# Which slot of a recurrent step takes filler work: a one-core scheduler change in a four-layer residual block

## The chip, the cores and the metric

The kernel runs on one core of one Trainium2 chip. Its time is the device time of one execution in microseconds, and the figure for a kernel is the median over several executions. The profile is one further execution, recorded by the hardware profiler.

## The reference

The input x has shape (8, 512, 256): 8 sequences of 512 time steps with 256 features, and there is one condition vector of 256 features per sequence. Four layers follow each other, each added to its input:

```
x = x + L0(x, cond)   # 8 routed experts (top 2 by a sigmoid router), one shared expert
x = x + L1(x, cond)   # Haar wavelet down and up, gated: reduces to a scale per sequence and feature
x = x + L2(x, cond)   # x@base_down + low rank of rank 8, gelu, base_up + low rank
x = x + L3(x, cond)   # a GRU over time:
   Z = sigmoid(xz + H@Whz.T + bhz);  R = sigmoid(xr + H@Whr.T + bhr)
   H_tilda = tanh(xh + (R*H)@Whh.T + bhh)
   H = Z*H + (1-Z)*H_tilda;          Y = H@Whq.T + bhq
```

All is float32. Layers 0 to 2 work on each time step alone; L3 is 512 steps that each need the step before.

## The kernel before

The 512 time steps are cut into 16 windows of 32 steps (256 columns: 8 sequences by 32 steps). For each window the lower layers (0 to 2) are a list of small jobs, made by `window_jobs` (routing by `route`): a PE job, here called a unit, is four matmuls that fill the four 32-column groups of the array, nearly always with 256 columns. ACT, DVE and POOL jobs stand between the units. Layer 3 then runs over chunks of 16 steps.

The order of all engines is fixed while the program is written (`tc.manual_schedule()`). The loop over steps emits the recurrent chain of each step, and at fixed places it calls `jobs.fill(engine, now, most)`, which takes up to `most` jobs that are ready by the planner's own clock (`STEP` = 2.43 us for a step, a time for each job in `TAKES`, a margin of 0.2 us). The program's order is then final: an engine that meets a job whose input is late stands still, with all that is queued behind it.

One step emits on PE, in this order:

1. eight matmuls into `grh` from the state `s_h` (reset gate, called R below) and eight into `gz` from `s_h` (update gate),
2. the first slot: units of `jobs.fill("PE", now + 0.5, ...)`, and in every second step four matmuls of the input projection of a later step (`wx` into `grh`, called P below),
3. eight matmuls into `grh` from `s_rh` (the candidate, called H below),
4. the second slot: in the other steps four projection matmuls into `gz`, called `Zx` below, and then units of `jobs.fill("PE", now + 1.44, ...)`.

Between them ACT makes `r`, `z` and `c`, and DVE transposes them, makes `s_rh` and, with two scans at line 1372, the new state `s_h`. After the scans DVE takes one or two jobs of the lower layers, and POOL one. ACT takes one after `z` and one after `c`. The next step's R waits for the scans. So the time from one pair of scans to the next is the length of a step.

The function `behind(s)` says whether more units are left than a straight line over the steps allows. Before the change the first slot takes a unit if `behind(s)`, the second takes two in every second step if `behind(s)`, and one otherwise. Output products of the GRU (`hist` times `Whq`, lines 453 and 1178, made by `output_jobs`) of chunks 0 to 11 are urgent jobs; those of the last four chunks (`HELD` = 12) lie in the queue `jobs.last`, which `fill` opens when no other PE job is left.

The activations `sig` of the lower layers lie in one ring of three buffers, `r_sig`, and a ring is given out in the order of asking. PSUM banks are rings too: `hp` has two, `low`, `acc` and `misc` one each. An `hp` unit that starts a bank therefore waits for the readers of the bank's former content.

Of the kernel before, what the change touches and what calls it, by code (L numbers as in the profile page):

```python
# [16 lines left out]
P = 128  # L17
B, T, C = 8, 512, 256
KC = C // P
# [7 lines left out]
NT = B * WS  # L27
# [109 lines left out]
class Jobs:  # L137


    def __init__(self):  # L140
        self.queues = {e: [] for e in TAKES}
        self.urgent = {e: [] for e in TAKES}
        self.last = {e: [] for e in TAKES}
        self.small = {e: [] for e in TAKES}
        self.clock = {e: 0.0 for e in TAKES}
        self.now = 0.0

    def add(self, eng, fn, deps=(), lazies=(), takes=None, queue=None, lag=0.0):
        job = Job(eng, fn, list(deps), list(lazies), takes, lag)
# [7 lines left out]
    def fill(self, eng, now, most, ahead=40, then=None, of=None):  # L157

        n = 0
        while n < most:  # L160
            last = [] if self.left("PE") else self.last[eng]
            for q in of or (self.urgent[eng], self.queues[eng], last):
                job = next((j for j in q[:ahead] if j.ready(now)), None)
                if job is not None:
                    break
            else:
                return n
            q.remove(job)
            made = job.emit(now)
            if then is not None:  # L170
                then(made)
            now += job.takes
            n += 1
        return n
# [25 lines left out]
def cond_resid_kernel(  # L200
# [29 lines left out]
    nc = tc.nc  # L230
# [31 lines left out]
    def ring(name, shape, bufs, space=None):  # L262
        return Ring(pool_of("r_" + name, bufs, space), name, shape, bufs)
# [4 lines left out]
    r_acc = ring("acc", pair, 1, PSUM)  # L268
    r_m = ring("misc", pair, 1, PSUM)
    r_sig = ring("sig", [P, NT], 3)  # L270
    r_lin = ring("lin", [P, NT], 2)
    r_g = ring("g", [P, NT], 6)
    r_gl = ring("gl", [P, NT], 3)
# [36 lines left out]
    jobs = Jobs()  # L310
# [31 lines left out]
    xw, xg, got_x = [], [], []  # L342
# [122 lines left out]
    def window_jobs(w, routed, xt, via_pool=False):  # L465
# [74 lines left out]
        for m in range(HC):  # L540
            h, sig, lin, g = bank(), Lazy(r_sig), Lazy(r_lin), Lazy(r_g)
# [28 lines left out]
        for e2 in range(0, E, 2):  # L570
            h = bank()
            for n in range(2):
                e = e2 + n
                j = hidden(h, n, lambda k, e=e: rw1_sb[:, k, e, :], got_rw1)
# [109 lines left out]
        ends = adapted(mid_ps, 0, x2, A_DOWN, done, True)  # L684
        mids = []
        for m in range(KC):
            sig = Lazy(r_sig)

            a = add(
                "ACT",  # L690
                lambda m=m, sig=sig: nc.scalar.activation(
                    sig.get(), mid_ps.get()[:, m], AF.Erf, scale=0.5 * RSQRT2
                ),
                [ends[m]],
                [mid_ps, sig],
            )
            mids.append(
                add(
                    "DVE",
                    lambda m=m, sig=sig: stt(  # L700
                        mid.get()[:, m], sig.get(), 1.0, mid_ps.get()[:, m], ALU.add, ALU.mult
                    ),
                    [a],
                    [mid_ps, sig, mid],
                )
            )
# [25 lines left out]
    def pe(fn, deps, lazies=(), takes=0.3):  # L732
        return jobs.add("PE", fn, deps, lazies, takes)
# [7 lines left out]
    def flat(z):  # L741
        t = z.get()
        return t if len(t.shape) == 2 else t.rearrange("p a b -> p (a b)")
# [45 lines left out]
    def route(ws, tiles, psum, via_pool, behind=()):  # L789

        first, n, J = ws[0], len(ws), B
        assert n == NQ and WS == 32
        takes = 0.18 + J * E / 1000.0
        logits = Lazy(psum)

        def products():
            for k in range(KC):
                for i, w in enumerate(ws):
                    nc.tensor.matmul(
                        flat(logits)[ts(i, 32), :NT],  # L800
                        rout_sq[:, k],
                        xw[w][:, k],
                        start=(k == 0),
                        stop=False,
                        skip_group_check=True,
                    )

        d = pe(
            products, [*(got_x[w] for w in ws), got_rout_sq, *behind], [logits], 0.45
        )  # L810

        def rt(name, last=E):
            return tiles.tile([P, J, last], F32, name=f"{name}_{first}")

        def bc(t):
            return t.broadcast_to([P, J, E])


        logit, s, sel, rank = rt("logit"), rt("s"), rt("sel"), rt("rank")
        turned = tiles.tile([P, B, 32], F32, name=f"turned_{first}")  # L820
        rb3 = rbias.rearrange("p (o e) -> p o e", o=1)
        pr3 = prio.rearrange("p (o e) -> p o e", o=1)

        def turn(dst, src):
            nc.vector.transpose(dst, src.rearrange("p (b q) -> p b q", q=32))

        d = dve(lambda: turn(turned, flat(logits)[:, :NT]), [d], [logits], 0.45)
        d = dve(lambda: tt(logit, turned[:, :, :E], tbias, ALU.add), [d, got_tbias], (), takes)
        d = act(lambda: nc.scalar.activation(s, logit, AF.Sigmoid), [d])

        def then(fn):
            nonlocal d
            queue = jobs.queues if via_pool else jobs.small
            d = jobs.add("DVE", fn, [d, got_rbias], (), takes, queue)

        then(lambda: tt(sel, s, bc(rb3), ALU.add))
        hot = []
        for i in range(2):
            top, best, one = rt(f"top{i}", 1), rt(f"best{i}", 1), rt(f"one{i}")
            then(lambda top=top: nc.vector.tensor_reduce(top, sel, AX.X, ALU.max))  # L840
            then(lambda top=top: tt(rank, sel, bc(top), ALU.is_equal))
            then(lambda: tt(rank, rank, bc(pr3), ALU.mult))
            then(lambda best=best: nc.vector.tensor_reduce(best, rank, AX.X, ALU.max))
            then(lambda one=one, best=best: tt(one, rank, bc(best), ALU.is_equal))
            hot.append(one)
            if i == 0:
                then(lambda one=one: stt(sel, one, -3.0e38, sel, ALU.mult, ALU.add))
        both = hot[0]
        den, some, rden = rt("den", 1), rt("some", 1), rt("rden", 1)
        then(lambda: tt(both, hot[0], hot[1], ALU.add))  # L850
        then(lambda: tt(s, s, both, ALU.mult))
        then(lambda: nc.vector.tensor_reduce(den, s, AX.X, ALU.add))
        then(lambda: nc.vector.tensor_scalar(some, den, EPS_GATE, None, ALU.is_gt))
        then(lambda: nc.vector.tensor_scalar(den, den, EPS_GATE, None, ALU.add))
        then(lambda: nc.vector.reciprocal(rden, den))

        then(lambda: stt(rden, rden, 0.5, some, ALU.mult, ALU.mult))
        then(lambda: nc.vector.tensor_scalar(some, some, -0.25, 0.25, ALU.mult, ALU.add))
        then(lambda: tt(s, s, bc(rden), ALU.mult))
        then(lambda: tt(both, both, bc(some), ALU.mult))  # L860
        square = squares[first // EARLY % 2]
        then(lambda: tt(square[:, :, :E], s, both, ALU.add))
        cT = tiles.tile([P, NT], F32, name=f"cT_{first}")
        d = dve(
            lambda: turn(
                cT.rearrange("p (b q) -> p b q", q=32), square.rearrange("p b q -> p (b q)")
            ),
            [d],
            (),
            0.45,  # L870
        )
        made = []
        for i in range(n):
            eng = "SP" if not via_pool else "ACT" if i else "POOL"

            def put(i=i, eng=eng):
                {"SP": nc.sync, "ACT": nc.scalar, "POOL": nc.gpsimd}[eng].dma_start(
                    out=comb_d[ws[i]], in_=cT[32 * i : 32 * i + E]
                )

            made.append(jobs.add(eng, put, [d], (), 0.9 if eng == "POOL" else 0.5, lag=LAG))
        return made
# [203 lines left out]
    with (  # L1086
# [158 lines left out]
        def behind(s, by=0):  # L1245
            return (
                any(j.done is None for j in ends[1])
                or jobs.left("PE") > all_left * (LAST - s) / (LAST + LEAD) + by
            )

        def late(s):

            return not jobs.left("PE")

        copying = None
        z_bias = None
        biased = []
# [6 lines left out]
        for c in range(NTC):  # L1264
            hist = hists[c]
            gates = upcoming
            for t in range(TC):
# [72 lines left out]
                if 2 * GS <= ahead < T:  # L1340
# [4 lines left out]
                    part = parts.pop(0)  # L1345
                    if ahead % WS == WS - 1:
                        projected[ahead // WS].done = now + 1.0
                jobs.fill("PE", now + 0.5, 1 if behind(s) or late(s) else 0)
                if part is not None and ahead % 2 == 0:
                    part()  # L1350
                    part = None
# [5 lines left out]
                cand, act_c = gate(rh[:, n, 1], AF.Tanh, "c", KC)  # L1357
                if part is not None:
                    part()
                two = behind(s, 8) or ahead % 2 == 0 and behind(s)  # L1360
                jobs.fill("PE", now + 1.44, 2 if two else 1)
                if bias_parts and t >= 7:
                    biased.append(bias_parts.pop(0)())
                    if not bias_parts:
# [100 lines left out]
```

## Time and profile before

| what | value |
|---|---|
| median of three runs | 1330.2 us (1329.89, 1330.2, 1331.93) |
| the profiled execution's own time | 1334.46 us |
| its span, first to last instruction | 1332.2 us |
| mean granted TensorE clock | 0.984 |
| PE busy | 1183.3 us (89%) |
| DVE busy | 914.9 us (69%) |
| ACT busy | 507.3 us (38%) |
| POOL busy | 149.3 us (11%) |
| first and last scan start (DVE, line 1372) | 71.1 us and 1326.5 us |

The profiled execution is 4.3 us above the median of the runs, so its parts cannot be taken for those of a typical run without a thought. Busy shares say little here: PE is busy nine tenths of the time, but much of that is filler that lies in gaps of the recurrent chain. What counts is how long a step takes, and which steps take longer than the others.

### The profile page before, as it was taken

How to read it: one execution, taken by the hardware profiler on the slowest of the kernel's cores; microseconds unless marked ns; L12 is line 12 of the kernel's file. 1: busy time of each engine (PE TensorE's matmuls, PEld its weight loads, DVE VectorE, ACT ScalarE, POOL GpSimd, SP SyncE). 2: the span in 40 equal slices, each digit the busy share in tenths (PEclk: the TensorE clock that was granted, in tenths of full speed). 3: DMA queues.
4: the chain of work that ended last, by engine and by line, in shares of the span. 5: the costliest groups of instructions: out<-in, count | busy, mean ns of one | idle time of the engine just before them, and what ended most of it. 6: DMA issues, size and time to landing. Idle time of an engine off the chain costs nothing.

```text
span 1332.2 us, 88576 instructions
## 1 busy us (share of the span) xinstructions
PE 1183.3 (89%) x39016; PEld 704.9 (53%) x39016; DVE 914.9 (69%) x6255; ACT 507.3 (38%) x3403; POOL 149.3 (11%) x228
## 2 busy tenths in 40 slices
PE   8999989999898998989898988888888888988885
PEld 4565555555555555555454554545454554555554
DVE  5267777777776767666676767667676766767665
ACT  2143433343343434334343434434343443433332
POOL 3310111101010110101011010101101010110000
PEclk8999999999999999999999999999999999989997
DMA  9910001101010000201000010100001000000111
GB/s 338 330 51 13 4 6 44 44 5 36 5 41 15 20 20 4 52 4 28 12 21 20 4 36 4 28 12 20 20 4 36 4 4 4 5 4 4 36 36 19
DMA packets 41586, 46.44 MB, mean 35 GB/s; under 512 B 27472, under 2 KB 31088, under 8 KB 40048
## 3 DMA queue, kind: packets, MB, share of 16 engines
q1 hardware_dynamic: 38304, 38.31, 9.6%
q8 instruction: 304, 4.98, 1.5%
q0 software_dynamic: 1184, 2.31, 0.6%
q14 instruction: 82, 0.67, 0.2%
q10 hardware_dynamic: 1712, 0.16, 0.1%
HBM read 36.45 MB, written 4.33 MB: 31 GB/s over the span
## 4 chain that ended last, share of the span: by engine, by line
PE 68%; DVE 17%; ACT 8%; issue 5%; DMA 1%; POOL 0%; DVEq 0%; ACTq 0%; POOLq 0%
PE grh L1115 34%; PE hp L453 13%; PE acc L453 8%; DVE rT L1295 6%; DVE d L1295 5%; PE gz L1115 5%; ACT r L1281 5%; PE low L453 4%; ACT c L1281 3%; PE misc L453 3%; DVE s_h L1372 2%; DVE s_rh L1312 2%; DMA brow<-in_bias_rows_dram 0%; DMA bc<-comb_d 0%; PE misc L1023 0%
## 5 line engine op out<-in xcount | busy, mean ns | idle before, releaser
L1281 ACT ACTIVATE r<-grh 128x32 f32<-128x32 f32 x1024 | 146.3, 195 | 439.8 <-PE grh L1115 439.8
L1295 DVE STREAM_TRANSPOSE rT<-r 128x32 f32<-128x32 f32 x1024 | 156.0, 190 | 225.6 <-ACT r L1281 221.6
L1115 PE MATMUL grh<-wh,s_h 128*32 128x64 f32 x8192 | 223.8, 226 | 75.4 <-DVE s_h L1372 74.2
L1115 PEld LDWEIGHTS grh<-wh,s_h 128*32 128x32 f32 x8192 | 145.0, 110 | 274.4 <-DVE s_h L1372 271.2
L1115 PE MATMUL grh<-wh,s_rh 128*32 128x64 f32 x8192 | 223.1, 227 | 52.0 <-DVE s_rh L1312 29.8
L1281 ACT ACTIVATE c<-grh 128x32 f32<-128x32 f32 x1024 | 146.3, 195 | 310.0 <-PE grh L1115 307.6
L1115 PEld LDWEIGHTS grh<-wh,s_rh 128*32 128x32 f32 x8192 | 141.6, 109 | 201.5 <-DVE s_rh L1312 198.9
L1295 DVE STREAM_TRANSPOSE d<-c 128x32 f32<-128x32 f32 x1024 | 156.5, 192 | 119.3 <-ACT c L1281 113.5
L1115 PE MATMUL gz<-wh,s_h 128*32 128x64 f32 x8192 | 212.1, 221 | 1.2 <-issue 1.2
L1115 PEld LDWEIGHTS gz<-wh,s_h 128*32 128x32 f32 x8192 | 155.3, 111 | 1.7 <-issue 1.6
L453 PE MATMUL hp<-x,sw_sb 128*32 128x256 f32 x2016 | 151.8, 389 | 1.7 <-ACT sig L546 1.1
L594 POOL TENSOR_TENSOR g<-gl,bc 128x256 f32<-128x256 f32 x128 | 93.6, 733 | 518.1 <-DVE s_h L1372 355.6
L453 PE MATMUL hp<-x,rw_sb 128*32 128x256 f32 x2016 | 149.6, 380 | 2.3 <-ACT sig L578 1.1
L453 PE MATMUL acc<-g,rw_sb 128*32 128x256 f32 x2048 | 150.2, 379 | 1.6 <-POOL g L594 1.1
L1372 DVE TENSOR_TENSOR_SCAN s_h<-d,d 128x16 f32<-128x16 f32 x1024 | 145.3, 183 | 0.0
L1312 DVE TENSOR_TENSOR s_rh<-rT,s_h 128x8 f32<-128x8 f32 x1024 | 133.1, 167 | 0.0
L1295 DVE STREAM_TRANSPOSE zT<-z 128x64 f32<-128x64 f32 x512 | 121.6, 238 | 1.1 <-ACT z L1281 1.1
L1281 ACT ACTIVATE z<-gz 128x64 f32<-128x64 f32 x512 | 121.0, 236 | 1.9 <-PE gz L1115 1.4
L1115 PE MATMUL grh<-wx,xt 128*32 128x128 f32 x2048 | 106.8, 276 | 3.3 <-ACT r L1281 3.3
L1386 ACT COPY hist<-s_h 128x16 f32<-128x16 f32 x512 | 105.9, 207 | 0.5 <-DVE s_h L1372 0.5
L1324 DVE TENSOR_TENSOR d<-zT,s_h 128x16 f32<-128x16 f32 x512 | 90.8, 177 | 17.6
L1325 DVE TENSOR_SCALAR d<-zT 128x16 f32<-128x16 f32 x512 | 86.8, 170 | 0.0
(151 smaller groups left out, 1193.4 us busy)
## 6 DMA issues: line engine op xcount, KB each, us to landing
bc<-comb_d SPq DMA_DIRECT2D x56, 256.0 KB, 3.2
w<-in_w_dram SPq DMA_DIRECT2D x8, 1024.0 KB, 12.6
out_dram<-x SPq DMA_DIRECT2D x14, 256.0 KB, 3.2
x<-in_xT_dram SPq DMA_DIRECT2D x2, 1536.0 KB
rw_sb<-in_rw_dram SPq DMA_DIRECT2D x2, 1024.0 KB
bc<-comb_d POOLq DMA_DIRECT2D x8, 256.0 KB, 8.4
sw_sb<-in_sw_dram SPq DMA_DIRECT2D x3, 512.0 KB, 6.3
wsq_a<-in_sq_a_dram SPq DMA_DIRECT2D x1, 1280.0 KB
```

The source lines that it names most:

```text
L453: nc.tensor.matmul(out[ts(j, 32)], lhs[:, ts(j, 32)], rhs, start=start, stop=False, skip_group_check=True,)
L594: lambda gl=gl, g=g, e=e: nc.gpsimd.tensor_tensor(g.get(), gl.get(), bcs[e // 2].get()[:, e % 2], ALU.mult),
L1115: nc.tensor.matmul(out[ts(j, 32)], lhs, rhs[:, ..., ts(j, FQ)], start=start, stop=False, skip_group_check=True,)
L1281: nc.scalar.activation(x, y, func)
L1295: ins = nc.vector.transpose(dst.rearrange("p i u b -> p i (u b)"), src.rearrange("p (i r) -> p i r", r=32),)
L1312: prod = tt(s_rh[u][:, k, u, :], rT[:, k, u, :], h[:, k], ALU.mult)
L1324: tt(d1[:, :, u, :, 1], zT[:, :, u, :], h, ALU.mult)
L1325: nc.vector.tensor_scalar(d0[:, :, :, 1], zT[:, :, u, :], -1.0, 1.0, ALU.mult, ALU.add)
L1372: new = nc.vector.tensor_tensor_scan(s_h[v][:, k, v].rearrange("p b w -> p (b w)"), d0[:, k].rearrange("p b w -> p (b w)"), d1[:, k, u].re ...
L1386: nc.scalar.copy(hist[:, :, t, :], s_h[v][:, :, v, :, 1])
```

## The change

Four things are done.

- The activations of layer 2 (the `sig` of `mid`) get a ring of their own with two buffers, `r_mid_sig`; they no longer take turns in `r_sig`.
- The router's product for four windows, one PE job of eight matmuls, becomes two jobs of four, one for each half of the features.
- The number of units of a slot depends on how many PE jobs are ready by the planner's clock. The first slot takes one if the kernel is behind and more than one is ready, else none; once all PE jobs of the lower layers are out, it takes an output unit only if more of them are left than steps. The second takes two if the kernel is behind and more than two are ready, else one. While window 1 is unfinished, and when the end has begun, the ready count isn't asked for.
- The end begins when the last product of layer 0 is out, not when no PE job is left: `fill` then opens `jobs.last`, and the held output units are spread over both slots of the remaining steps.

```diff
+        self.ending = lambda: not self.left("PE")
...
-            last = [] if self.left("PE") else self.last[eng]
+            last = self.last[eng] if self.ending() else []
...
+    r_mid_sig = ring("mid_sig", [P, NT], 2)
...
-            sig = Lazy(r_sig)
+            sig = Lazy(r_mid_sig)
...
-        def products():
-            for k in range(KC):
-                for i, w in enumerate(ws):
...
+        def products(k):
+            for i, w in enumerate(ws):
...
+        d = None
+        for k in range(KC):
+            deps = [*(got_x[w] for w in ws), got_rout_sq, *behind, d]
+            d = pe(lambda k=k: products(k), deps, [logits], 0.45)
...
+        def first_slot(s, at):
+
+            if any(j.done is None for j in ends[1]) or jobs.ending() and jobs.left("PE"):
+                return 1
+            if jobs.left("PE"):
+                return 1 if behind(s) and jobs.ready("PE", at + 1.0) > 1 else 0
+            return 1 if len(jobs.last["PE"]) > T - s else 0
+
+        def second_slot(s, at):
+
+            if not jobs.left("PE"):
+                return 1
+            two = behind(s, 8) or (s + 5) % 2 == 0 and behind(s)
+            if two and (any(j.done is None for j in ends[1]) or jobs.ending()):
+                return 2
+            return 2 if two and jobs.ready("PE", at + 1.0) > 2 else 1
+
+        jobs.ending = lambda: l0_ends[-1].done is not None
...
-                jobs.fill("PE", now + 0.5, 1 if behind(s) or late(s) else 0)
+                jobs.fill("PE", now + 0.5, first_slot(s, now + 0.5))
...
-                two = behind(s, 8) or ahead % 2 == 0 and behind(s)
-                jobs.fill("PE", now + 1.44, 2 if two else 1)
+                jobs.fill("PE", now + 1.44, second_slot(s, now + 1.44))
```

More of the change, by code (lines that the diff above doesn't have):

```diff
@@ L794, in route @@
         logits = Lazy(psum)
-        def products():
-            for k in range(KC):
-                for i, w in enumerate(ws):
[L799 to L810, printed above, removed]
+        def products(k):
+            for i, w in enumerate(ws):
+                nc.tensor.matmul(
+                    flat(logits)[ts(i, 32), :NT],
+                    rout_sq[:, k],
+                    xw[w][:, k],
+                    start=(k == 0),
+                    stop=False,
+                    skip_group_check=True,
+                )
+        d = None
+        for k in range(KC):
+            deps = [*(got_x[w] for w in ws), got_rout_sq, *behind, d]
+            d = pe(lambda k=k: products(k), deps, [logits], 0.45)
         def rt(name, last=E):
@@ L1249, in behind @@
             )
-        def late(s):
-            return not jobs.left("PE")
+        def first_slot(s, at):
[12 more added lines that the diff above has]
+        jobs.ending = lambda: l0_ends[-1].done is not None
         copying = None
```

## The prediction

> **What bounds the kernel now.** I read the cores' line first, then the page, the waits, a timeline of the scans, and tables of stretches. The page says PE 89% busy, but the waits say what the time hangs on:
>
> ```profile
> span 1332.2 us, 88576 instructions
> ACT r L1281 <- PE grh L1115: 439.8, 509, 3.3
> ACT c L1281 <- PE grh L1115: 307.6, 487, 1.5
> PEld grh L1115 <- DVE s_h L1372: 271.2, 501, 1.0
> PEld grh L1115 <- DVE s_rh L1312: 198.9, 479, 0.7
> ```
>
> PE to ACT to DVE to PE, about 500 times each: the chain of one step goes round the engines, and the filler lies in PE's gaps. So I took the length of every step, from the timeline of the line 1372 scans, end to end: 1255.3 us for 511 steps, and the commonest length is 2.417 us. A step with two lone units in its second slot and one in its first has the median 2.417, and so has a step with none. Filler is free as long as it is on time. 511 x 2.417 is 1235.1, so **20.2 us of the profiled run are excess**, and the change can win no more than that and the ends. I sorted the excess by step:
>
> - 5.4 us: steps 80-81, 142-143, 206-207 and 457-459, each just after a light stretch.
> - 5.6 us: steps 55-56, 72, 74, 97, where PE waits for "issue".
> - 1.6 us: steps 508 to 511.
> - 7.6 us: some sixty steps of 0.04 to 0.6 each, where a slot is too full or a unit late.
>
> The first group and the third have one cause. Stretches of 3.41 us, two pairs, then the two at the end:
>
> ```profile
> 421.96:425.37 3.41, 1.76 (x90) 1.17 (x81) 2.72 (x19) 1.84 (x12) 0.00 (x0) 1.00 0.03 5
> 425.37:428.79 3.42, 3.42 (x70) 2.44 (x74) 1.81 (x12) 0.74 (x6) 0.00 (x0) 0.50 0.02 5
> 578.97:582.39 3.42, 1.76 (x90) 1.17 (x81) 2.73 (x19) 1.84 (x12) 0.00 (x0) 1.00 0.02 5
> 582.39:585.80 3.41, 3.41 (x68) 2.41 (x72) 1.75 (x11) 0.64 (x5) 0.00 (x0) 0.50 0.00 0
> ...
> 968.09:971.50 3.41, 1.79 (x76) 1.24 (x76) 2.85 (x20) 1.64 (x11) 0.00 (x0) 1.00 0.02 5
> ...
> 1312.84:1316.25 3.41, 1.74 (x80) 1.26 (x80) 1.94 (x15) 1.15 (x10) 0.00 (x0) 1.00 0.04 10
> 1316.25:1319.67 3.42, 2.28 (x82) 2.01 (x85) 2.02 (x16) 1.03 (x8) 0.00 (x0) 0.50 0.00 0
> ```
>
> The columns are length, PE busy, weight loads, DVE, ACT, POOL, granted clock, DMA. A stretch with PE busy 1.74 to 1.76 of 3.41 us is followed by one at half clock; one with 1.78 or 1.79 is not. The clock's changes lie on a grid of 3.413 us. A step of the bare recurrence has 1.1 us of PE, 1.55 in a stretch: under the line. In matmul columns, counting both passes of float32, it has 3072 a step, the drops follow stretches of 5312 or less, and the lightest middle stretch without one has 5376. Two empty slots in a row, of steps 141 and 142, let the clock fall, if the grid lies badly.
>
> Two more costs, a slot too full and the instruction stream:
>
> ```profile
> 137.24 1.05 PE L799 MATMUL misc<-x,rout_sq 128*32 128x256 f32 x16
> 138.10 0.61 PE L453 MATMUL hp<-x,sw_sb 128*32 128x256 f32 x8
> 138.53 0.41 PE L1115 MATMUL grh<-wh,s_h 128*32 128x64 f32 x16
> ...
> 198.77 1.78 SPq L485 DMA_DIRECT2D bc<-comb_d  x4
> ...
> 205.64 1.07 PE L453 MATMUL low<-u,low_out 128*32 128x256 f32 x16 [2.15 <-issue]
> ```
>
> The scan before R ended at 138.24 and R began at 138.53, 0.3 late (on time it begins 0.04 before that end), behind router plus unit. In the third case four 256 KB transfers are issued together, no 16 KB packet of the instruction queue starts from 195.5 to 203.2 (3.5 to 5 us apart else), and PE runs dry.
>
> **The change part by part.** I counted slots in the two programs' orders. The matmuls are the same 19512, none is added.
>
> *Empty slots.* Before, 41 second slots hold no unit (20 of them with Zx), after 18, and most pairs of empty slots (21-22, 45-46, 51-52, 75-76, 109-111, 140-142, 172-174, 204-206, 236, 267, 300, 365, 397, 455-459) now hold a unit each. What was put there was taken from full slots. I slid the 3.413 us grid in 64 positions over each order, counted columns, and took 5340 as the line. Before: 2.1 half-clock stretches up to step 500, on average over the positions; after: 0.2 (step 469 alone). The profiled run drew five (two of them one pair), for 5.38 us: 1.1 each. So the part is 5.4 less 0.2 = **-5.2 in this execution**, and -2.1 in a typical run: three stretches fewer are also most of what sets the 1334.46 above the 1330.2.
>
> Here the Trainium skill speaks against the change. "TensorE: Matmul & The Clock Gate", section "What's actually happening", has the PE fall back after at least one idle window of about 3.4 us, and the section on oscillation asks for no PE gap above that. The longest gap in the loop is 2.15 us, and before 425.37 PE was never idle for a microsecond. By that rule empty slots cost nothing, the part is 0, and the end gains nothing. The rows show half clock at half activity, so I go with them; by the rule the sum would be 3.3 less.
>
> *End.* Steps 506-507 before hold little, and the last outputs are 32 columns wide: half clock from 1316.25. After, outputs begin at step 459 and last with a unit or two a step to 507, then 64-column units in 508-509. Sliding the grid: 3.0 half-clock stretches from step 500 before, 0.8 after. 1.56 x 0.8 / 3.0 leaves 0.4: **-1.2**. Behind the last scan the same three instructions stand on ACT, PE, DVE and the same two stores: 0, or -0.3 with the clock up. DVE's last-slice adds and SP's stores move with the outputs; SP has nothing else by then, the last inputs being in.
>
> *Full slots and late units.* By pattern, from the step lengths:
>
> - Router. Three steps of eight router matmuls plus a unit (28, 58, 88): +0.297, +0.299, +0.299. After, two of the three still have both halves in one slot, without a third unit; the third is split. A slot of two units costs 0: -0.9. A second job instead of one adds nothing on other engines.
> - Two output units with Zx before P: 29 steps of 0.047 (R at 1249.60 is such a one, 0.06 late). Nine are left: -0.94.
> - Zx, `acc`, `hp` and then a `gl` that waits for that `hp`: seven steps of 0.18 to 0.28, 1.67 together, since the next first slot's `hp` waits for `gl`, and P and H stand behind it. One is left: -1.43.
> - The same with `hp` before `acc`, six steps, 0.31; two left: -0.2. Without Zx, ten steps of 0.094; seven left: -0.28.
>
> That is -3.75. Against it stand pairs that the trace doesn't show: a slot of two with a `mid_sig` after it, `gl` behind two `hp` units, three DVE jobs in one gap (one step). Below nothing is possible only by what these replace, already counted. Upper bound: a dozen such places at 0.25, the late `gl`'s price, is 3. I take 1.2, as most of them have the distance of places that cost 0: **-2.5**. The three claims matmuls' step (4, +0.55) stays.
>
> *Prologue.* PE has two units more before step 0. One (0.43 x 2 for both halves) goes ahead of `misc<-mid`, where PE stood 0.38 waiting for `mid`: +0.4 on the way to `xt`. Behind it, a wait of 0.57 for `sig` (66.29) goes, and P, which starts at 67.61 though `xt` was there at 66.24, comes sooner. Bounds -1.0 and +0.5, **-0.3**.
>
> *Instruction stream and transfers.* SP's order: the second routing's four stores and the four `bc` loads still go together, at steps 54-55 in place of 52-54; so the 3.15 us stall and its half-clock follower (0.62) I leave in place. The other three (0.48, 0.53, 0.86) sit behind single loads in the busiest steps; which steps get them shifts. **0**; bounds -5.6 (none) and +2 (the burst lasts 6.35 us, a dry PE of 4 in place of 2.15).
>
> *Sum* against the profiled execution: 1334.46 - 5.2 - 1.2 - 2.5 - 0.3 = 1325.3. Against the median: 1330.2 - 2.1 - 1.2 - 2.5 - 0.3 = 1324.1. After the change the draw of the grid matters little, so both should name one number: **1324.5**.
>
> **The rivals.**
>
> - *First-slot units wait.* A unit in the first slot stands ahead of H, on the chain. After, 40 first-slot `hp` units need a bank whose reader is DVE's job of the gap just before, 25 one whose reader is ACT's job after `c`; before 45 and 10. At 0.25 each, all 65 would be +16, less the 1.7 already there: 1338. It beats the gain from 25 waits on, and is slower by 0.2% from 35 on. For: the seven steps named. Against: those are 7 of 45; a first DVE job ends 0.45 into the step and the slot starts at 0.5. 7%.
> - *A draw.* A typical run has few drops, the burst's stall grows by 2 and new waits reach 3: 1330.2 - 3.3 - 3.75 + 3 + 2 = 1328. 13%.
> - *The clock follows the skill's rule*, or another line: -2.8, 1327.4. 10%, half of it within 0.2%.
> - *The split router does not split*: true in two of three steps, but the gain comes from the third unit's absence. No time of its own.
>
> **How the numbers follow.** The main case has 70%. A measurement of this kernel can tell 0.2%, 2.7 us. Low end: no new waits (-1.2) and half of the stalls gone (-3): 1320. High end: new waits at 3 (+1.8), a longer burst (+2), prologue at +0.5 (+0.8): 1329. This holds the draw and the skill's rule. Faster (under 1327.5): 70% and most of the rule's tenth and a bit of the draw, 0.80; same 0.13; slower 0.07.
>
> **What would show it.** Right: granted clock near 1.00 from 75 to 1310 save after the burst; scans 2.417 apart around steps 141, 205, 457; no 0.3 at the router's steps; the output steps at 2.417. Wrong: waits of H for `gl` or `sig` in the first slot in dozens of steps; half-clock stretches in spite of filled slots; a stall at step 55 of over 4 us; a first scan later than 72.

## The result, and the profile after

The changed kernel takes 1320.17 us (median of 4 runs) against 1330.86 us for the kernel before: ratio 0.9911, interval 0.9899 to 0.9924. A second set of runs of it gave 0.9899 (0.9883 to 0.9915); all its 9 runs have a median of 1320.6 us. The forecast of 1324.5 us had the direction and most of the places right, and took the gain for half of what it is: 5.7 us below the median that it started from, against 10.7 us measured.

The two profiled executions are 1334.46 and 1319.46 us. First the span from the page after, and four rows of the waits of after (us in total, times, longest):

```profile
span 1317.7 us, 88546 instructions
```

```profile
ACT r L1298 <- PE grh L1117: 426.6, 505, 7.3
PEld grh L1117 <- DVE s_h L1388: 308.7, 511, 1.0
ACT c L1298 <- PE grh L1117: 307.8, 501, 1.0
...
PEld grh L1117 <- DVE s_rh L1329: 190.8, 480, 0.8
```

The chain still goes round PE, ACT, DVE, PE, and the common step is 2.417 us as before. But PE now waits for the new state in 511 steps and for 308.7 us, where before it waited in 501 and for 271.2: it arrives early more often, because fewer slots run over.

The stretches of 3.41 us around steps 141 and 142, and those at the end (length, PE busy, weight loads, DVE, ACT, POOL, granted clock, DMA):

```profile
412.80:416.21 3.41, 3.06 (x112) 1.81 (x108) 2.68 (x19) 1.74 (x12) 0.00 (x0) 1.00 0.02 5
416.21:419.63 3.42, 3.05 (x107) 1.59 (x102) 2.58 (x17) 1.39 (x9) 0.00 (x0) 1.00 0.02 5
...
1307.09:1310.51 3.42, 1.92 (x108) 1.40 (x98) 2.17 (x17) 1.29 (x10) 0.00 (x0) 1.00 0.02 5
1310.51:1313.92 3.41, 1.13 (x56) 0.79 (x56) 1.53 (x10) 0.49 (x3) 0.00 (x0) 0.99 0.02 5
1313.92:1317.33 3.41, 0.00 (x0) 0.00 (x0) 0.00 (x0) 0.00 (x0) 0.00 (x0) 0.50 0.34 38
```

Of all stretches from 78 to 1307 us the lightest has 1.99 us of PE; none falls to 1.76. The clock is full from 16.8 to 1313.9 us, two microseconds after the last scan has ended (1311.66). A stretch with 1.92 us does not lower it.

Which waits of PE went, between 76 and 1305 us; before:

```profile
PE low L453 <- issue: 2.2, 1, 2.2
PE gz L1115 <- issue: 1.2, 3, 0.6
PE grh L1115 <- issue: 0.6, 1, 0.6
PE hp L453 <- issue: 0.5, 1, 0.5
PE acc L453 <- issue: 0.4, 1, 0.4
...
PEld hp L453 <- DVE gl L586: 2.8, 11, 0.3
...
PEld hp L453 <- ACT sig L546: 1.7, 9, 0.2
...
PEld hp L453 <- ACT sig L578: 0.4, 2, 0.2
```

and after:

```profile
PE acc L455 <- issue: 0.7, 1, 0.7
PE gz L1117 <- issue: 0.6, 1, 0.6
...
PEld hp L455 <- DVE gl L588: 0.8, 4, 0.2
PEld hp L455 <- ACT sig L548: 0.8, 4, 0.3
...
PEld hp L455 <- ACT sig L580: 0.2, 1, 0.2
```

The `issue` rows of PE, in which it runs dry with no partner to wait for, add up to 4.9 us before and 1.3 after. The waits of `hp` units for `gl` and `sig` are 4.9 us in 22 places before and 1.8 us in 9 after.

To compare executions I sorted the excess of each step, its length less 2.4175 us, into four kinds: steps from 500 on ("end"), steps in which PE runs dry by over 0.2 us ("dry"), other steps with half clock ("half"), and all others ("rest": full slots and late units). The sums of each kind, rounded, in us, for one profiled execution of each run, with the end of the first pair of scans (the runs are told below; shift means more PE instructions at the start):

| kernel | first scans | half | dry | rest | end | sum |
|---|---|---|---|---|---|---|
| before, the profile shown | 71.4 | 6.0 | 5.6 | 6.7 | 1.7 | 19.9 |
| before, second execution (b_same) | 72.9 | 4.5 | 6.4 | 7.5 | 1.7 | 20.0 |
| b_shift64 | 71.6 | 7.8 | 2.7 | 7.2 | 1.7 | 19.4 |
| b_shift128 | 73.5 | 6.1 | 3.4 | 8.6 | 1.7 | 19.7 |
| b_shift192 | 74.3 | 4.2 | 3.5 | 6.7 | 1.7 | 16.0 |
| b_warm | 71.9 | 0 | 4.4 | 8.8 | 0.3 | 13.5 |
| b_paced | 72.4 | 3.9 | 1.0 | 7.3 | 1.7 | 13.9 |
| b_warmpaced | 72.4 | 0 | 0 | 9.6 | 0.3 | 10.0 |
| b_router | 71.9 | 4.1 | 1.5 | 6.3 | 1.7 | 13.6 |
| b_midsig | 73.9 | 1.2 | 2.6 | 4.4 | 1.7 | 9.9 |
| a_noslots | 72.1 | 0 | 1.3 | 4.5 | 2.7 | 8.5 |
| a_norouter | 72.5 | 0 | 2.3 | 5.0 | 0 | 7.3 |
| after, the profile shown | 72.3 | 0 | 1.0 | 3.1 | 0 | 4.1 |
| after, second execution (a_same) | 72.6 | 0 | 1.4 | 3.5 | 0 | 4.9 |
| a_shift64 | 72.1 | 0 | 3.7 | 3.0 | 0 | 6.7 |
| a_shift128 | 71.8 | 0 | 3.1 | 3.6 | 0 | 6.7 |
| a_shift192 | 74.1 | 0 | 1.5 | 3.2 | 0.4 | 5.2 |
| a_paced | 73.9 | 0 | 1.2 | 3.8 | 0.4 | 5.4 |

### The profile page after: what moved, and what is told of

Same layout as the page of the kernel before. It is cut to its first block, busy times and chain, and to the rows that moved or that the text cites. A ratio compares the mean times of both kernels' runs of the same rounds, so it can differ in the third digit from the quotient of the medians.

```text
span 1317.7 us, 88546 instructions
## 1 busy us (share of the span) xinstructions
PE 1182.9 (90%) x39016; PEld 682.1 (52%) x39016; DVE 914.0 (69%) x6255; ACT 507.2 (38%) x3403; POOL 149.3 (11%) x228
## 4 chain that ended last, share of the span: by engine, by line
PE 67%; DVE 19%; ACT 9%; issue 4%; DMA 0%; ACTq 0%; DVEq 0%
PE grh L1117 36%; PE hp L455 11%; PE acc L455 7%; DVE d L1312 7%; DVE rT L1312 6%; ACT c L1298 5%; PE gz L1117 5%; ACT r L1298 4%; PE low L455 4%; DVE s_h L1388 3%; PE misc L455 3%; DVE s_rh L1329 2%; PE misc L1025 1%; DMA b<-in_bias_dram 0%; ACT sig L548 0%
## 5 line engine op out<-in xcount | busy, mean ns | idle before, releaser
L1117 PEld LDWEIGHTS grh<-wh,s_h 128*32 128x32 f32 x8192 | 139.9, 109 | 308.7 <-DVE s_h L1388 308.7
L1117 PEld LDWEIGHTS grh<-wh,s_rh 128*32 128x32 f32 x8192 | 138.7, 108 | 194.6 <-DVE s_rh L1329 190.8
L1117 PE MATMUL gz<-wh,s_h 128*32 128x64 f32 x8192 | 208.9, 219 | 0.7 <-issue 0.6
```

The lines of the kernel that those rows point to most:

```text
L1117: nc.tensor.matmul(out[ts(j, 32)], lhs, rhs[:, ..., ts(j, FQ)], start=start, stop=False, skip_group_check=True,)
```

## The experiments

Names with b_ start from the kernel before, those with a_ from the changed one.

### The two costs that change from run to run: clock and dry PE

**b_same**: no edit.

> The kernel before once more, unchanged: what of its excess is fixed by the program's order and what is drawn anew. Theory: the half-clock stretches come from the lie of the 3.41 us grid, so this execution has other ones in the middle than steps 80, 142, 206, 457 (on average 2.1 of them, 1.1 us each), and always the last steps from about 508; the instruction stall at step 55 (3.15 us) and the full slots (router steps 28, 58, 88 at +0.30) stay within 0.1 us. Rival: the stall at step 55 is drawn as well, and moves by over 1 us. Time 1330.9, within 1.5.

Measured: 1334.38 us, ratio 0.9997 (0.9982 to 1.0012). The clock's stretches lie elsewhere (at 272.9, 347.9, 505.0, 583.5, 1194.5 us), and the stall of step 55 cost 1.1 us in place of 3.15; others came instead. So the sizes are drawn anew in each execution; the rival came true. The kernel before scatters accordingly: 88 runs of it over all comparisons have a median of 1333.4 us, the middle eight tenths from 1330.5 to 1336.7, and the runs with a lower granted clock are the longer ones (24 runs at 0.985 or less have a median of 1335.5 us, ten at 0.990 or more one of 1331.6). The three runs that the forecast had (1330.2) lie at the low end. Of the 84 runs of the later comparisons only 24% are as short as the longest of the four of the first one (1331.93), so four such runs in a row would be rare by chance, and a difference between the occasions is not excluded.

**b_warm**: in each slot that takes no unit, four or eight matmuls on zeros. Every result stays the same.

```diff
+        def warm(out, gate):
+            across(out[:, (n - 1) % NG], zeros[:, 0:32], wx[:, 0, gate])
...
-                jobs.fill("PE", now + 0.5, 1 if behind(s) or late(s) else 0)
+                if not jobs.fill("PE", now + 0.5, 1 if behind(s) or late(s) else 0):
+                    warm(rh, RH)
...
-                jobs.fill("PE", now + 1.44, 2 if two else 1)
+                if not jobs.fill("PE", now + 1.44, 2 if two else 1):
+                    warm(z, G_Z)
+                    warm(z, G_Z)
```

> The kernel before with four or eight matmuls of zero weights put into each slot that got no unit, into a part of the gate bank that nobody reads any more (they add zero, the outputs stay). Theory, clock by activity: no half-clock stretch in the middle and none or a late one at the end, so 2.1 x 1.1 + 1.6 = 3.9 us less than before, about 1327. Rival, the clock falls only after an idle stretch of 3.4 us: nothing to win, and the added matmuls can only cost, 1331 to 1332.

Measured: 1330.82 us, ratio 0.9977 (0.9964 to 0.9991), 3.1 us less. Its stretches around steps 141 and 142, in the columns of above:

```profile
415.78:419.19 3.41, 2.51 (x120) 2.03 (x120) 2.41 (x18) 2.10 (x12) 0.00 (x0) 1.00 0.02 5
419.19:422.61 3.42, 2.90 (x108) 1.97 (x112) 3.11 (x19) 1.13 (x9) 0.00 (x0) 1.00 0.02 5
```

Where before's stretch held 1.76 us of PE and half clock followed, there are 2.51 us, zeros among them, and the clock stays full. It does so from 16.4 to 1323.7 us. With more work on PE and nothing else touched, all half-clock stretches of the loop are gone, and most of the end's cost. This settles the forecast's first step: activity sets the clock here, and the rule that only an idle window lowers it does not describe this kernel. What it is worth in time is less sure. In the table half and end fall by 7.1 us against the mean of the five executions of before's order, while the rest rises from 7.3 to 8.8 with the zeros, which would leave 5.6; the runs show 3.1 (1.2 to 4.8 by the interval). The profiled execution of b_warm (1328.11 us) is the fastest of its runs, and the zeros also move PE's instructions, so the difference is not settled.

**b_paced**: SP's transfer of a step waits for the scans of the step before, so that transfers come one at a time.

```diff
-                jobs.fill("SP", now, 1)
+                jobs.fill(
+                    "SP", now, 1, then=lambda made: after(made, paced) if paced else None
+                )
...
+                paced = new
```

> The kernel before, but each transfer that SP issues in the loop waits for the scans of the step before the one it was planned for, so that the four loads of the gates of window 8 no longer go together. Theory, the burst of 1 MB holds up the instruction packet of PE: the 3.15 us stall at step 55 and the half-clock stretch after it (0.6) are gone, 1330.9 - 3.7 = 1327. Rival, the packet is late for another reason (PE asks too late): the stall stays within 0.5 us, 1331.

Measured: 1332.2 us, ratio 0.9982 (0.9966 to 0.9998), 2.4 us less by the ratio, 1.7 by the medians. Its `issue` rows between 76 and 1305 us:

```profile
PE acc L453 <- issue: 0.9, 2, 0.7
PE hp L453 <- issue: 0.4, 1, 0.4
PE grh L1115 <- issue: 0.2, 1, 0.2
```

1.5 us are left of 4.9 and 6.2, and the stall of step 55 is gone. So most dry stretches come from transfers that crowd together. An example from the timeline of b_same (start, length, instruction, and in brackets PE's idle time before it):

```profile
555.24 6.87 SPq L485 DMA_DIRECT2D bc<-comb_d  x2
...
561.51 0.64 PE L453 MATMUL acc<-g,rw_sb 128*32 128x256 f32 x8 [1.37 <-issue]
```

The loads and stores filled 555.08 to 559.71 with 766 KB. PE's instruction packet before had started at 552.73, the next at 559.25, 6.5 us later in place of some 4.2, and PE went on 2.3 us after that.

**a_paced**: the same edit in the changed kernel.

> The changed kernel with the same pacing of SP. There was no stall at step 55 in its profile although its four loads went together, so the theory of the burst has nothing to win there: 1320.2, within 1. If the changed kernel's runs without a profile do have the stall, it gets 3 us faster: 1317.

Measured: 1320.86 us, ratio 0.989 (0.986 to 0.9919); `issue` 1.2 us. Nothing is gained in time: with 1.3 and 1.6 us of `issue` in the changed kernel as it stands, there is little left to take.

**b_warmpaced**: both edits in the kernel before.

> The kernel before with both remedies at once: matmuls on zeros in its empty slots (no half clock) and transfers that wait for the scans of the step before (hardly a dry PE). Theory (clock and dry stretches add up, and the rest of the change's gain is in full slots and late units): ratio 0.996, about 5.5 us, against 0.990 of the changed kernel; 'issue' under 2.5 us and the clock full to 1305 us. Rival (the two costs hide each other, or the rest is also clock and instructions): ratio 0.992 or less, or no better than 0.9977, that of the zeros alone.

Measured: 1326.26 us, ratio 0.995 (0.9935 to 0.9965), 6.6 us less. Clock and dry PE do add up:

```profile
PE gz L1115 <- issue: 0.2, 1, 0.2
```

This is the only dry row left (b_warm, with the same PE instructions and free transfers, has 4.4 us of dry steps), and the clock is full until after the last scans. The changed kernel is still 5.7 us faster. That distance is in the rest (9.6 against 3.3): full slots and late units, and the price of the zeros.

### What each part of the change does

**b_midsig**: the own ring for the activations of `mid`, nothing else.

```diff
+    r_mid_sig = ring("mid_sig", [P, NT], 2)
...
-            sig = Lazy(r_sig)
+            sig = Lazy(r_mid_sig)
```

> The kernel before, with the own ring for the lower layers' activations alone. In the program its empty second slots fall from 41 to 21, and by the sliding grid the half-clock stretches up to step 500 from 2.1 to 0.6. Theory (the ring does most of it): the clock stays full to about step 455 (-2), and with the units spread more evenly PE runs dry for 1 to 3 us of 'issue' instead of 4 to 6 (-3): about 5 us less than before, ratio 0.996. Rival (the ring gives the clock alone, and the dry stretches go by another part): ratio 0.9985, 'issue' 4 to 6.

Measured: 1325.91 us, ratio 0.994 (0.9924 to 0.9956), 8 us less, more than either side expected. Two lines give over half of the gain. The slots' counts in the code are as before; what is ready when a slot asks has changed. Empty second slots fall from 41 to 21, and from 15 us, where the start's half clock ends, to 1182 us only one stretch of half clock is left, at 38.6, ahead of the first step. The pair of steps 457 and 458, which hold almost no unit, remains: half clock from 1182.0 to 1188.9 us. The rest falls from 7.3 to 4.4. The dry part, 2.6, is within what before's order shows at other places of the packets.

**b_router**: the split product, nothing else (the diff's hunk at `products`).

> The kernel before, with the router's product in two units alone. Theory: the three steps of +0.30 go (-0.9), the empty slots and 'issue' stay (4 to 6 us); ratio 0.9993. Rival: shifting all later units by one place evens the queue as the ring does: 'issue' under 3 us and ratio 0.997.

Measured: 1330.61 us, ratio 0.9974 (0.9962 to 0.9985), where the theory had 0.9993; the rival's numbers came, `issue` under 3 us too. The three steps of 0.30 account for 0.9 us; the rest sum went down by just 1.0. What is more is in dry (1.5) and half (4.1), the two drawn kinds, so I read this as 1 us for the part and the remainder as undecided; the rival is not refuted.

**a_noslots**: own ring, split product and opened end, with the old counts of units.

> The old unit counts of both slots (one in the first if behind, two in every second step in the second), with the three other parts of the change kept: own ring for the lower layers' activations, router's product in two units, end opened by the last product of layer 0. Theory: the count by ready units does the main work, so here the light slots and with them the half-clock stretches stay (about 2 us), PE still runs dry for about 5 us of 'issue' between 76 and 1305 us, and the full slots stay; what goes is the end (-1.3) and the router's three steps (-0.9): about 1328.7. Rival: the dry stretches of PE come from the order of the loads, which the three other parts also shift: 'issue' falls to 1 to 2 us here too, and the time is about 1325.

Measured: 1325.59 us, ratio 0.9938 (0.9919 to 0.9956). The theory that the ready count does the main work is wrong: without it the clock already is full to 1291 us and `issue` is 1.5 us. But it is no faster than the ring alone. Opening the end without spreading it moves the output units forward and leaves the second slots of steps 502 and 503 without a unit: half clock from 1291.4 to 1298.2 us, and an end of 2.7 in place of 1.7. From here to the changed kernel (1320.6) the two slot functions give 5 us: 2.7 at the end, 1.2 of the rest, and a remainder that no single profile shows. They were not run alone.

**a_norouter**: the changed kernel with the product of four windows in one unit.

```diff
-        d = None
-        for k in range(KC):
-            deps = [*(got_x[w] for w in ws), got_rout_sq, *behind, d]
-            d = pe(lambda k=k: products(k), deps, [logits], 0.45)
+        d = pe(
+            products, [*(got_x[w] for w in ws), got_rout_sq, *behind], [logits], 0.45
+        )
```

> The changed kernel with the router's product of four windows in one unit of eight matmuls again. Theory: where such a unit shares a slot with another, the step is 0.30 us longer, three times: +0.9, about 1321.1; the rest of the profile as in the changed kernel. Rival: with the slots given out by the ready count, the double unit rarely has company, or the other units that come after it move too: 0 to +0.3, not to be told from the changed kernel.

Measured: 1323.16 us, ratio 0.9921 (0.9902 to 0.994), about 2.6 us above the changed kernel by the medians, with overlapping intervals. Steps 28, 57 and 87 are 0.30, 0.41 and 0.41 longer. One of them:

```profile
138.42 1.05 PE L801 MATMUL misc<-x,rout_sq 128*32 128x256 f32 x16
139.15 0.28 DVE L1388 TENSOR_TENSOR_SCAN s_h<-d,d 128x16 f32<-128x16 f32 x2
139.28 0.61 PE L455 MATMUL hp<-x,rw_sb 128*32 128x256 f32 x8
...
139.71 0.41 PE L1117 MATMUL grh<-wh,s_h 128*32 128x64 f32 x16
```

The scans end at 139.43, and R starts at 139.71 behind the third unit. In the changed kernel, where two halves fill the slot, R starts at its time:

```profile
208.70 1.05 PE L800 MATMUL misc<-x,rout_sq 128*32 128x256 f32 x16
209.32 0.28 DVE L1388 TENSOR_TENSOR_SCAN s_h<-d,d 128x16 f32<-128x16 f32 x2
209.57 0.43 PE L1117 MATMUL grh<-wh,s_h 128*32 128x64 f32 x16
```

R starts 0.25 after the scans do, in a_norouter 0.56. That is the mechanism of the forecast, at its size. The three steps make 1.1 us; the remainder of the 2.6 is within the scatter, and this profile has a stall of 1.29 us at step 55.

### Is it the order, or where the packets lie?

PE's instructions reach it in packets over DMA queue 8. The page after has 305 of them, 5.00 MB together, and PE has 39016 matmuls and as many loads: 256 instructions to a packet. If a dry PE depends on where the packets' borders meet the bursts, then some more instructions at the very start must change it. The first two groups of matmuls on zeros were cut by columns, so that their columns stay the same and 64, 128 or 192 instructions come on top, quarters of a packet:

```diff
-    claim(gz.rearrange("p c n f -> p (c n f)"))
-    claim(rh0)
+    claim(gz.rearrange("p c n f -> p (c n f)"), 2)
+    claim(rh0, 4)
```

(2 and 2 for 64, 4 and 4 for 192; the number is into how many parts the columns are cut.)

> The changed kernel, with the first two groups of matmuls on zeros cut in columns into two and four (same columns, 128 more PE instructions at the very start): PE's instruction packets of 256 instructions then fall half a packet elsewhere in the steps. Theory: that PE no longer runs dry is a matter of where the units are; 'issue' stays at 1 to 2 us and the time within 0.7 us of 1320.2. Rival: it is a matter of how the packets happen to lie against the bursts of the loads; half a packet on, 'issue' is 3 to 6 us again, and the time 1322 to 1325.

> The kernel before, with the same 128 more PE instructions at the start. Theory (place of the units): 'issue' between 76 and 1305 us stays at 4 to 6 us, the time within 1 us of 1330.9. Rival (where the packets lie): 'issue' changes by 2 us or more either way, with the stall of step 55 gone or larger, and the time follows it.

> The changed kernel as it is, another execution. Theory: ratio 0.991 again, 'issue' between 76 and 1305 us at 1 to 3 us, under the 4.2 of the lowest execution of a kernel with the shared ring and free transfers. Rival: the 1.3 us of its first profile were luck; 'issue' 4 to 6 us in this one.

> The changed kernel with 64 more PE instructions at the very start (both first groups on zeros cut in two by columns), a quarter of an instruction packet. Theory (the level is set by the units' places, the draw adds about one us): 'issue' 1 to 3 us, ratio within 0.001 of the changed kernel's. Rival (all is where the packets lie): one of the shifts shows 4 us or more, with a ratio of 0.994.

> The kernel before with 64 more PE instructions at the start (the same edit as in the changed kernel's). Theory (the units' order of before makes PE run dry wherever its packets lie): 'issue' 4 to 6 us. Rival (a draw of where the packets lie, in which before stands badly and the changed kernel well): 'issue' 1.5 to 3.6 us, as in the changed kernel's shifts.

> The kernel before with 192 more PE instructions at the start, three quarters of a packet. As for 64: theory 4 to 6 us of 'issue'; rival 1.5 to 3.6 us.

> The changed kernel with 192 more PE instructions at the start. Theory: 'issue' 1 to 3.6 us as in the other three places of its packets (1.3 and 1.6 unshifted, 3.6 at 64, 3.0 at 128). Rival (no difference between the two orders but the draw): 4 us or more in this fourth place.

| place of the packets | before: us, ratio, issue | changed: us, ratio, issue |
|---|---|---|
| 0 | 1334.38, 0.9997, 6.2 (4.9 in the profile shown) | 1320.78, 0.9899, 1.6 (1.3) |
| 64 | 1332.08, 0.9991, 2.5 | 1321.4, 0.9906, 3.6 |
| 128 | 1332.54, 0.9994, 4.2 | 1322.49, 0.9919, 3.0 |
| 192 | 1334.66, 1.0015, 4.0 | 1322.53, 0.9922, 1.3 |

At 64 the order is turned round: here b_shift64, then a_shift64.

```profile
PE gz L1117 <- issue: 1.7, 2, 1.1
PE hp L455 <- issue: 0.4, 1, 0.4
...
```

```profile
PE gz L1119 <- issue: 2.6, 3, 1.1
PE hp L457 <- issue: 0.6, 1, 0.6
...
```

The theory that before's order makes PE dry wherever its packets lie has fallen (2.5 at 64). So has "all is luck" in its plain form, since none of the changed kernel's five executions reaches 4, though at 128 it was the rival's numbers that came (3.0 us of `issue`, 1322.49 us). The times of the runs do not follow the `issue` column, which is from one execution each: at 192 the changed kernel has its least `issue` and, with 128, its longest times. Over the five executions of each, the dry steps cost 4.3 us on average in before's order (2.7 to 6.4) and 2.1 in the changed one (1.0 to 3.7), a difference of 2.2. At the place where both kernels happen to stand, the difference is 4.8. So, as far as so few profiles tell, about half of what the changed kernel saves here is a matter of where its packets lie and of the execution. The other half may be the order, but with ranges that overlap this is not settled.

## Why the prediction was right in direction and half in size

The forecast's sum against the profiled execution was 9.2 us; the two profiles differ by 15.0. Against the median it was 6.1 us (1330.2 to 1324.1); the runs differ by 10.7. The step that failed is the instruction stream, entered as 0: the two profiles differ there by 4.6 us, the means of five by 2.2. Behind it come two terms of the right mechanism and the wrong size: the empty slots of a typical run and the new waits in full slots. By the forecast's own steps:

| step | forecast | the two profiles | mean of five executions each |
|---|---|---|---|
| empty slots, clock | -5.2 | -6.0 | -5.7 |
| instruction stream | 0 | -4.6 | -2.2 |
| full slots and late units | -2.5 | -3.6 | -4.1 |
| end | -1.2 | -1.7 | -1.6 |
| prologue | -0.3 | +0.9 | -0.2 |

The stretch from the last scans to the end of the span, forecast at 0 or -0.3, is not in the table: it has 5.6 us in the profile before and 6.0 in the one after.

- **Empty slots** were right in mechanism and nearly in size for the profiled execution, and b_warm shows the cause. Wrong was the "typical run" with -2.1. It rested on the sliding grid's 2.1 stretches. The five profiles of before's order had 3 to 6 between 76 and 1285 us, 5.2 on average. The traces show a good part of the reason: the line of 5340 columns was drawn from one profile, and it does not hold in the others. Of the 23 drops there, ten follow a stretch with more columns than that (one of them the stretch of step 55's stall), and eight follow one in which PE was busy for 1.80 to 1.90 us, which in the first profile seemed enough. One of them, from b_shift64, in the columns of above:

```profile
329.11:332.52 3.41, 1.90 (x92) 1.21 (x82) 2.03 (x17) 1.57 (x11) 1.11 (x2) 1.00 0.00 0
332.52:335.94 3.42, 3.42 (x70) 2.45 (x74) 1.22 (x11) 0.66 (x5) 0.00 (x0) 0.50 0.02 5
```

  This error hid because the median of the three runs was low as well: the count made the gain too small by 3.6 us, and the base lay 3.2 below the median of the 88 runs.
- **Instruction stream** is the step that failed: "I leave in place" for step 55, and "0" for the others. The burst of four `bc` loads is still there, and in the profile shown PE passes it without running dry. That is luck of this execution: in the other four of the changed kernel's order PE does run dry behind it, and the step concerned is 0.42 to 0.96 us too long. In a_same, the same program:

```profile
205.35 1.77 SPq L487 DMA_DIRECT2D bc<-comb_d  x4
...
210.59 0.32 PE L1117 MATMUL grh<-wh,s_h 128*32 128x64 f32 x8 [0.49 <-issue]
```

  In before's order step 55 is too long by 3.15 us in the profile shown and by 0.26 to 1.12 in the other four. The change stays inside the bound of -5.6. The forecast treated a stall as belonging to a burst, at a fixed size. Its size also depends on how a late packet falls against the burst, which the execution draws anew (b_same, a_same) and, as far as the shifts tell, a change that moves every unit as well. A value of 0 took before's draw, which was a bad one, as a fixture; the means of five differ by about -2.
- **Full slots**: the sum is -3.6 to -4.1, so gains of about the 3.75 came; of the five patterns only the router's was tried alone. The term of 1.2 against it, for new waits, is what was mis-sized. The waits of `hp` for `gl` and `sig` fell from 4.9 to 1.8 us; no dozen of places appeared. The claim of step 4 stayed (0.55), and step 88, one of the router's, still has 0.26.
- **Prologue**: the profiles' +0.9 says nothing. The end of the first scans lies between 71.4 and 74.3 us in one order as in the other, and the means differ by 0.2.

The first rival, waits in the first slot, is refuted by the wait rows above. The rival that the clock falls only after an idle window is refuted by b_warm; its branch "another line" is right in so far as the line of 5340 columns did not hold. The rival that the router doesn't split is right about the place, and a_norouter's timeline shows that the gain comes from the third unit's absence.

## What to carry to other kernels

When a scheduler fills slots, look first at what it finds ready: here two buffers of their own for one kind of activation gave 8 of 13 us, more than the rules of how many units to take. Split the excess over the common step into kinds, and test each kind by removing it alone (work on zeros for the clock, paced transfers for a dry PE); what is drawn anew in each execution must be entered with its mean, not with the one profile's value. Do not draw a line from one profile: the next ones crossed it. And a base of three runs can sit at the edge of the scatter.

## What the runs showed of the hardware

- PE's instructions come in packets of 16 KB, 256 instructions, about every 4.2 us. In the eighteen profiles there are 76 places between 76 and 1305 us where PE ran dry by over 0.25 us. Each ended 2.2 to 2.7 us after a packet had started, and at each of them at least 256 KB of other transfers had run in the 8 us before, which holds for only 30% of all moments of that stretch (before; 31% after). The packets themselves took 1.1 us on average, with or without company: it is their start that comes late (6.5 us after the one before in the example of b_same).
- The granted clock halves after 3.41 us stretches in which PE was busy for 1.76 us, though it was never idle for a microsecond there. In the eighteen profiles, from 76 us to the last change of the clock, every stretch with 1.77 us or less was followed by half clock and none with 1.91 or more; of those between, 15 were and 22 were not, so something beside PE's busy time decides there, which stays open. Zeros multiplied in otherwise empty slots were enough to hold the clock (b_warm).
